# A four-layer graph network on one core: tail rows and the next head's row sent in pieces behind feature loads, and the order of some sigmoids and scalings

## Chip, core and metric

The kernel runs on one core of a Trainium2 chip. The metric is the device time of one execution in microseconds (us); 1734.3 us is the median of three runs of the kernel before, which lie between 1733.95 and 1735.32 us.

## What is computed

The input is a feature matrix `x` of 2708 x 512 and a symmetric 0/1 adjacency matrix `adj` of 2708 x 2708. Four graph layers follow one another, each on a layer norm with relu of the running `x`, and each added to it. The change lies in the third one, graph attention with eight heads of 64 columns:

```python
h = jnp.maximum(_layernorm(x, axis=-1), 0.0)
Wh = jnp.einsum('nd,hdo->hno', h, W)             # 8 heads, 64 columns each
f1 = jnp.einsum('hno,ho->hn', Wh, a1)
f2 = jnp.einsum('hno,ho->hn', Wh, a2)
e = leaky_relu(f1[:, :, None] + f2[:, None, :], negative_slope=0.2)
e = jnp.where(adj[None, :, :] > 0, e, NEG_INF)
attention = softmax(e, axis=-1)
x = x + elu(einsum('hnm,hmo->hno', attention, Wh))   # heads side by side
```

The other three layers are matrix products with `adj` and with 512 x 512 weights. They are untouched.

## The kernel before

**Engines.** TensorE (PE) multiplies matrices, VectorE (DVE) and ScalarE (ACT) work on tiles element by element, GpSimd (POOL) issues one kind of DMA here, and SyncE (SP) issues most of the others. Each engine works through its own list of instructions in order. The lists are written by a recording layer from the order in the source; a call inside `tc.issue_after(x)` is placed behind the instruction `x` in its lists.

**Steps.** The 2708 nodes are cut into `NC` = 22 chunks, 21 of 128 rows and a last one of 20. Attention goes through ten units: unit 0 and unit 1 are head 0 on the first 1408 and the last 1300 columns, units 2 to 7 are heads 1 to 6 on all 2708 columns, units 8 and 9 are head 7, again in two parts. A unit has 22 steps, one for each chunk; units 1 to 8 begin with the chunk of 20 rows. Steps are counted through: unit 0 has steps 0 to 21, unit 1 steps 22 to 43, unit 2 begins with step 44.

**One step.** `scale` (ACT, L1110 and L1112) multiplies the chunk's features `wh` by a factor of each row and writes `whs` (4 buffers). `make` (DVE, L1126) forms the tile `t`, the larger of the head's row `rb` and a value of each partition, times the adjacency; four buffers of it exist (`TILES`), so the DVE may be up to four steps ahead of the PE, and `t` of step s waits until the PE has multiplied `t` of step s-4. `multiply` (PE, L1385) multiplies `whs` by `t` into `av` and, in some steps, `sums`. In the others (17 of the 22 in units 1 to 8) `compare` (ACT, L1144) writes the tile `b` by a steep sigmoid of `t`, and `multiply_sides` adds its product to `sums` one step later. The loop of steps calls `load_wh(s + 6)` where a group of three chunks begins, then `scale(s + 3)`, `make(s + 3)`, `compare(s + 1)`, `multiply(s)` and `multiply_sides(s - 1)`.

**What else runs in steps 1 to 42.** `mask` has POOL load pieces of a stored 0/1 mask (`maskd`, 162 or 176 KB each), two pieces for each half of 17 chunks, into five buffer places that take turns; `count_neighbors` multiplies them (PE, `adj_sums`, L1464) one step after the planned load. A load waits until the product that used its buffers has been done.

**The plan.** `behind(s, f, ...)` has `f` called at the end of step s of the loop. Of these calls the following matter. `load_row1` (SP, L1038) sends one head's row of up to 2708 values to all 128 partitions of `rb` (1354 KB for a whole row; two buffers); unit 1's part is planned at step 10 and unit 2's whole row at step 24. `load_tails` at step 12 loads what the chunk of 20 rows needs in the six heads of units 2 to 7, packed into 120 partitions: besides small pieces, for each head its row on 20 partitions of `tails_row` (L1056, 212 KB each). `exp_tails` (step 20, ACT) and `make_tails` (step 36, DVE, L1074) turn them into one tile of 120 x 2708, which takes the place of `t` in the first step of units 2 to 7. `evict` (ACT, L1429, with SP's L1431) copies a unit's results out after its last step.

`load_wh` (SP, L1096 and L1099) has three buffers of three chunks each. Its DMA for a group waits for the scalings of the group three before it.

Of the kernel before, what the change touches and what calls it, by code (L numbers as in the profile page):

```python
# [14 lines left out]
AF = mybir.ActivationFunctionType  # L15
# [7 lines left out]
R = 128  # L23
# [21 lines left out]
def fast_layers(  # L45
# [36 lines left out]
    nc = tc.nc  # L82
    N, D = x_in.shape
    H, _, O = w2.shape
    NC = -(-N // R)
# [3 lines left out]
    last_rows = N - (NC - 1) * R  # L89
    assert last_rows <= TAIL and TAIL + last_rows <= R  # L90

    def rows(c):
        return min(R, N - c * R)
# [250 lines left out]
    class Fusion:  # L344
# [34 lines left out]
        def multiply(self, i, f, k):  # L379
            if k == 0:  # L380
                self.po[i, f] = ps.tile([P, D], F32, name="fused_ps", tag="ps")
            po = self.po[i, f]
            nc.tensor.matmul(  # L383
                po,
                self.wsT[i][:, k, f * P : (f + 1) * P],
                self.wc[i][:, k, :],
                start=(k == 0),
                stop=(k == NF - 1),
            )
            if k == NF - 1:  # L390
                wf = self.pool.tile([P, D], F32, name="wf", bufs=1)
                nc.scalar.copy(wf, self.po.pop((i, f)))
                nc.gpsimd.dma_start(fused[i][f * P : (f + 1) * P, :], wf)
# [92 lines left out]
    rT = dram.tile([H, NC * R], F32, name="rT")  # L486

    with ExitStack() as ring_ctx:
# [31 lines left out]
        with tc.tile_pool(name="l0", bufs=2) as wk, ExitStack() as ctx_l0:  # L520
            units = [(g, m) for g in range(len(groups)) for m in range(NC)]
# [462 lines left out]
    STEEP = 2.0**62  # L984
# [3 lines left out]
    units = [(h, 0, N) for h in range(H)]  # L988
# [3 lines left out]
    middle = [units[u][0] for u in range(2, len(units) - 2)]  # L992

    def in_tails(u, m):
        return m == NC - 1 and units[u][0] in middle
# [7 lines left out]
    def by_side(u, m):  # L1003
        return 0 < u < len(units) - 1 and m in BY_SIDE
# [14 lines left out]
    eb = at.tile([R, NC, H], F32, name="eb")  # L1019
# [9 lines left out]
    row, weight, wh, whs, acc, sides, made, scaled = {}, {}, {}, {}, {}, {}, [], {}  # L1029
# [17 lines left out]
    def lines_of(h):  # L1047
        i = middle.index(h)
        return slice(i * last_rows, (i + 1) * last_rows)

    def load_tails():
        g, k = where[NC - 1]
        for i, h in enumerate(middle):
            own = lines_of(h)
            src = rT[h : h + 1, :N]
            nc.sync.dma_start(  # L1056
                tails_row[own],
                bass.AP(tensor=src.tensor, offset=src.offset, ap=[[0, last_rows], [1, N]]),
            )
            nc.sync.dma_start(tails_v[own], vT[g][:last_rows, k, :N])  # L1060
            nc.sync.dma_start(tails_f[own, :1], f12[:last_rows, NC - 1, H + h : H + h + 1])
            nc.sync.dma_start(
                tails_w[own, i, :O], whd[(NC - 1) * R :, h * O : (h + 1) * O]
            )
            nc.sync.dma_start(tails_w[own, i, O:], one6[:last_rows])
# [15 lines left out]
        )  # L1081

    GROUP = 3

    def load_wh(s):
        u = steps[s][0]
        h = units[u][0]
        t = at.tile([R, GROUP, O], F32, name="wh", bufs=3)
        ms = [m for v, m in steps[s : s + GROUP] if v == u and not in_tails(u, m)]
        full = [m for m in ms if m < NC - 1]  # L1090
        k = len(full)
        for j, m in enumerate(sorted(ms)):
            wh[u, m] = t[:, j]
        if k:
            src = whd[full[0] * R : (full[0] + k) * R, h * O : (h + 1) * O]
            nc.sync.dma_start(t[:, :k], src.rearrange("(k p) o -> p k o", p=R))  # L1096
        if k < len(ms):
            src = whd[(NC - 1) * R :, h * O : (h + 1) * O]
            nc.sync.dma_start(t[:last_rows, k], src)  # L1099

    def scale(s):

        u, m = steps[s]
        h, q = units[u][0], rows(m)
        if in_tails(u, m):
            whs[s] = tails_w[:LINES, middle.index(h)]
            return
        t = at.tile([R, O + S], F32, name="whs", bufs=4)
        by = ef[:q, m, h : h + 1]
        ins = nc.scalar.activation(t[:q, :O], wh.pop((u, m))[:q], AF.Copy, scale=by)  # L1110
        if not by_side(u, m):
            ins = nc.scalar.activation(t[:q, O:], one6[:q], AF.Copy, scale=by)  # L1112
        scaled[s] = ins.ins
        whs[s] = t[:q]

    def make(s):
        u, m = steps[s]
        h, lo, hi = units[u]
        q = rows(m)
        g, k = where[m]  # L1120
        if in_tails(u, m):
            weight[s] = tails_row[:LINES]
            made.append(made[-1])
            return
        t = at.tile([R, N], F32, name="t2", bufs=TILES)
        ins = nc.vector.scalar_tensor_tensor(  # L1126
            t[:q, : hi - lo],
            row[h][:q, lo:hi],
            ec[:q, m, h : h + 1],
            vT[g][:q, k, lo:hi],  # L1130
            op0=ALU.max,
            op1=ALU.mult,
        )
        weight[s] = t[:q]
        made.append(ins.ins)

    def compare(s):

        u, m = steps[s]
        h, lo, hi = units[u]  # L1140
        q = rows(m)
        if by_side(u, m):
            b = at.tile([R, N], BF16, name="b", bufs=2)
            nc.scalar.activation(  # L1144
                b[:q, : hi - lo],
                weight[s][:, : hi - lo],
                AF.Sigmoid,
                bias=eb[:q, m, h : h + 1],
                scale=STEEP,
            )  # L1150
            sides[s] = b

    l2p = ctx.enter_context(ExitStack())
# [104 lines left out]
    def rows2(c):  # L1258
# [12 lines left out]
        if c == LATE:  # L1271
            load_wh(0)
            load_wh(GROUP)
        if LATE < c <= LATE + 3:
# [14 lines left out]
    tails_row = tails.tile([P, N], F32, name="tails_row")  # L1289
# [121 lines left out]
    def multiply_sides(s):  # L1411

        if s in sides:
            u, m = steps[s]
            h, q = units[u][0], rows(m)
            b = sides.pop(s)[:q]
            at_col = (m * H + h) * 8
            w = parts[:q, at_col : at_col + S]
            four(acc[u][1], sizes_of(u)[1], [(w, b, j) for j in range(4)], s)
# [71 lines left out]
    def behind(s, fn, *args):  # L1491
        plan.setdefault(s, []).append((fn, args))
# [5 lines left out]
    behind(10, load_row1, *units[1])  # L1498
    behind(9, split, EARLY, NC)
    behind(12, load_tails)  # L1500
    behind(20, exp_tails)
    behind(36, make_tails)
    behind(3 * NC, load_l3_weights)
    behind(30, spread_nodes)
    for u in range(2, len(units)):
        if units[u][1] == 0:
            behind(max(1, u - 1) * NC + 2, load_row1, units[u][0], 0, N)
    for u in range(len(units)):
        behind((u + 1) * NC - 1, evict, u, 0)
        behind(min((u + 1) * NC, len(steps) - 1), evict, u, 1)  # L1510
# [34 lines left out]
    for s in range(len(steps)):  # L1545
        if s == (len(units) - 3) * NC + 1:
            tails_ctx.close()
            first3 = ctx.enter_context(
                tc.tile_pool(name="first3", bufs=1, side="right", reuse_waits="tile")
            )  # L1550
            rings3 = [first3]
            b3 = first3.tile([P, D], F32, name="b3")
            nc.sync.dma_start(
                b3, bass.AP(tensor=bias3.tensor, offset=bias3.offset, ap=[[0, P], [1, D]])
            )
            e3_ctx = ctx.enter_context(ExitStack())
            e3 = e3_ctx.enter_context(
                tc.tile_pool(name="e3", bufs=2, side="right", reuse_waits="tile")
            )
        if s + 6 < len(steps) and (s + 6) % NC % GROUP == 0:  # L1560
            load_wh(s + 6)
        if s + 3 < len(steps):
            scale(s + 3)
            make(s + 3)
        if s + 1 < len(steps):
            compare(s + 1)
        multiply(s)
        multiply_sides(s - 1)
        for fn, args in plan.pop(s, ()):
            if fn is load_l3_weights:  # L1570
                with tc.issue_after(row_loads[-1]):
                    fn(*args)
            elif fn in (spread_nodes, split):
                with tc.issue_after(made[s]):
                    fn(*args)
            elif fn is count_neighbors:
                with tc.issue_after(multiplied[s]):
                    fn(*args)
            else:
                fn(*args)  # L1580
# [674 lines left out]
def kernel(tc: tile.TileContext, *args: bass.AP):  # L2255

    nc = tc.nc
    with tc.tile_pool(name="verdict", bufs=1) as pool:
        verdict = pool.tile([1, 1], I32, name="verdict")
        fast_layers(tc, *args, verdict)  # L2260
        odd = nc.values_load(verdict[0:1, 0:1], min_val=0, max_val=P + 1)
        with tc.If(odd > 0):
            general_layers(tc, *args)
# [32 lines left out]
```

## Time and profile before

| | |
|---|---|
| runs of the kernel before | 1733.95, 1734.3, 1735.32 us |
| the profiled execution | 1735.47 us, of which the span of the trace is 1733.6 us; mean granted clock 0.997 |
| PE | busy 1715.0 us (99%) |
| DVE | busy 1307.8 us (75%) |
| ACT | busy 876.5 us (51%) |
| POOL | busy 276.6 us (16%) |
| `t` by L1126, DVE | x214, 511.8 us |
| `b` by L1144, ACT | x136, 308.3 us |
| attention steps | first `t` at 796.2 us, last at 1337.5 us from the span's start |
| mask loads | landed 2.5 to 13.5 us after their issue, median 3.8 us |

Times inside the trace are counted from the start of the span. In the timeline a row is one instruction, or several alike in a row (x and their number), with its start, its length, the engine, the line, the operation, output and inputs, shapes, and in brackets how long the engine was idle ahead of it and what ended that. Starts of neighbours may overlap the ends of the rows before by about 0.1 us, since an engine takes the next instruction in before the last has drained. SPq is SP's queue, whose rows are the issues of DMAs and not their transfers. PEclk is the granted clock of TensorE, 1.00 being full speed.

### The profile page before, as it was taken

To read this page: it belongs to the slowest core of one execution; us is meant where nothing else is said; L and a number is where in the kernel's file an instruction comes from. 1 tells how busy PE (TensorE), PEld (TensorE's weight loads), DVE (VectorE), ACT (ScalarE), POOL (GpSimd) and SP (SyncE) were. 2 spreads that over 40 slices of the span, in tenths; PEclk is the share of its full clock that TensorE was granted. 3 is DMA by queue.
4 is the path that set the end of the run, shared out by engine and by line. 5 is a ranking of instruction groups with operands and counts; after the bars stand their busy time and mean duration, and the time that the engine had idled before them with its cause. 6 is when DMAs were issued, how large, how long until landed. Compare 5 with 4: busy or idle time off the path is not lost.

```text
span 1733.6 us, 29645 instructions
## 1 busy us (share of the span) xinstructions
PE 1715.0 (99%) x11252; PEld 1018.8 (59%) x11252; DVE 1307.8 (75%) x1885; ACT 876.5 (51%) x1565; POOL 276.6 (16%) x314
## 2 busy tenths in 40 slices
PE   9999999999999999999899999999999999999998
PEld 5567777744458888644344433433434555588886
DVE  7759889855556666877799999999999777633334
ACT  5447767622224510265497888888894666400000
POOL 1003323312121111366320000000001222100000
PEclk9999999999999999999999999999999999999999
DMA  9336666444464421344771221122022444312221
GB/s 319 116 118 198 204 205 190 141 116 123 123 161 147 163 92 49 118 132 140 205 208 29 61 64 45 28 65 66 16 67 74 141 139 136 101 46 100 74 73 42
DMA packets 180846, 200.96 MB, mean 116 GB/s; under 512 B 86320, under 2 KB 117488, under 8 KB 179677
## 3 DMA queue, kind: packets, MB, share of 16 engines
q1 hardware_dynamic: 144156, 131.47, 27.0%
q10 hardware_dynamic: 28888, 45.68, 7.0%
q0 software_dynamic: 7648, 21.82, 3.9%
q8 instruction: 90, 1.47, 0.4%
q14 instruction: 64, 0.52, 0.1%
HBM read 123.42 MB, written 67.15 MB: 110 GB/s over the span
## 4 chain that ended last, share of the span: by engine, by line
PE 75%; DVE 14%; issue 6%; ACT 2%; DMA 2%; POOL 1%; DVEq 0%; SPq 0%; ACTq 0%; POOLq 0%
PE acc L437 37%; DVE t L1126 11%; PE nb_ps L193 8%; PE av L1385 8%; PE wh_ps L193 4%; PE self_ps L193 4%; PE line_ps L193 4%; PE h_ps L193 3%; PE hT_ps L258 2%; PE sums L1385 2%; PE fused_ps L383 2%; ACT b L1144 1%; DMA x<-maskd 1%; DMA x<-in_x 1%; PE av_ps L1320 1%
## 5 line engine op out<-in xcount | busy, mean ns | idle before, releaser
L1126 DVE SCALAR_TENSOR_TENSOR t<-rb,ec,vT 128x2708 f32<-128x2708 f32 (+2 forms) x214 | 511.8, 2465 | 13.2 <-PE sums L1385 10.4
L1385 PE MATMUL av<-t,whs 128*32 128x451 f32 (+4 forms) x4432 | 424.0, 515 | 5.6 <-DVE t L1126 2.8
L437 PE MATMUL acc<-halves,kt 128*128 128x512 f32 x1848 | 423.6, 390 | 1.0 <-DVE kt L928 1.0
L437 PEld LDWEIGHTS acc<-halves,kt 128*128 128x128 f32 x1848 | 346.0, 188 | 75.3 <-DVE kt L928 2.6
L1144 ACT ACTIVATE b<-t,eb 128x2708 bf16<-128x2708 f32 (+2 forms) x136 | 308.3, 2267 | 46.5 <-DVE t L1126 46.3
L1385 PEld LDWEIGHTS av<-t,whs 128*32 128x32 f32 (+1 forms) x4432 | 146.0, 110 | 200.0 <-issue 156.9
L437 PE MATMUL acc<-halves,ar 128*128 128x512 f32 x924 | 243.7, 414 | 0.0
L437 PEld LDWEIGHTS acc<-halves,ar 128*128 128x128 f32 x924 | 172.6, 188 | 58.2 <-issue 20.3
L928 DVE SCALAR_TENSOR_TENSOR kt<-lastr,index,vT 128x512 fp32r<-128x512 int16 (+3 forms) x154 | 108.5, 719 | 63.3 <-PE acc L437 62.1
L1613 DVE CAST kt<-vT 128x512 fp32r<-128x512 uint8 (+3 forms) x154 | 56.3, 368 | 130.8 <-PE acc L437 130.7
L1337 POOL TENSOR_SCALAR z<-y 128x512 f32<-128x512 f32 x22 | 44.2, 2007 | 559.0 <-DVE y L1330 548.3
L570 DVE TENSOR_TENSOR_SCAN cum<-ai,deg 128x512 int16<-128x512 int32 (+2 forms) x110 | 128.1, 1168 | 0.0
L235 ACT ACTIVATE ln_rs<-ln_mv,eps 128x1 f32<-128x1 f32 x88 | 25.6, 294 | 195.0 <-DVE ln_mv L230 192.8
L613 ACT ACTIVATE cum<-cum,limit 128x512 int16<-128x512 int16 (+3 forms) x132 | 88.0, 667 | 57.1 <-DVE deg L578 54.8
L1110 ACT ACTIVATE whs<-wh,ef 128x64 f32<-128x64 f32 x214 | 72.1, 342 | 51.2 <-PE sums L1385 21.0
L228 DVE BATCH_NORM_STATS2 ln_st<-x 128x6 f32<-128x512 f32 x88 | 60.4, 688 | 48.1 <-DMA x<-x 33.9
L920 ACT CAST hT<-vT 128x704 bf16<-128x704 uint8 (+1 forms) x68 | 50.8, 757 | 63.2 <-DMA maskd<-hT 51.7
L193 PE MATMUL h_ps<-w0s,hT 128*128 128x512 f32 x168 | 76.0, 595 | 0.6 <-DVE ln_rs L237 0.3
L193 PE MATMUL wh_ps<-w2s,hT 128*128 128x512 f32 x168 | 75.8, 594 | 0.0
L564 ACT ACTIVATE ar<-ai 128x512 fp32r<-128x512 int32 (+2 forms) x132 | 75.0, 568 | 1.6 <-DMA ai<-in_adj 1.1
L193 PE MATMUL self_ps<-wfs,hT 128*128 128x512 f32 x168 | 75.7, 593 | 0.0
L193 PE MATMUL nb_ps<-wfn,hT 128*128 128x512 f32 x168 | 75.6, 593 | 0.0
(223 smaller groups left out, 1957.0 us busy)
## 6 DMA issues: line engine op xcount, KB each, us to landing
x<-x SPq DMA_DIRECT2D x105, 256.0 KB
ai<-in_adj SPq DMA_DIRECT2D x84, 256.0 KB
x<-x ACTq DMA_DIRECT2D x84, 256.0 KB
x<-in_x SPq DMA_DIRECT2D x42, 256.0 KB
rb<-rT SPq DMA_DIRECT2D x7, 1354.0 KB
maskd<-hT ACTq DMA_DIRECT2D x34, 176.0 KB
wh<-whd SPq DMA_DIRECT2D x62, 96.0 KB
packed<-two POOLq DMA_DIRECT2D x44, 128.0 KB, 3.1
```

Of the source, the lines that this page charges most:

```text
L193: nc.tensor.matmul(po[:n], lhsT[:, f, :n], w[:, f, :], start=(f == 0), stop=(f == NF - 1))
L228: nc.vector.bn_stats(st[:n], xc[:n])
L437: nc.tensor.matmul(acc[:R], weight[:, k * R : (k + 1) * R], parts[:, i, :], start=(m == 0 and i == 0), stop=(m == NC - 1),)
L564: nc.scalar.activation(ar[:, :gw], ai[:, :gw], AF.Square, accum_out=squares[:R, m, g : g + 1])
L570: nc.vector.tensor_tensor_scan(cum[:n, :gw], ai[:n, :gw], ai[:n, :gw], 0.0 if g == 0 else deg[:n, m : m + 1], op0=ALU.add, op1=ALU.max,)
L613: nc.scalar.activation(cum[:n, :gw], cum[:n, :gw], AF.Sign, bias=limit[:n], scale=-1.0, accum_out=signs[:n, m, g : g + 1],)
L928: nc.vector.scalar_tensor_tensor(by_chunk(kt, cs), lastr[:, cs[0] * R : (cs[-1] + 1) * R].rearrange("p (c r) -> p c r", r=R), index[:R, m ...
L1110: ins = nc.scalar.activation(t[:q, :O], wh.pop((u, m))[:q], AF.Copy, scale=by)
L1126: ins = nc.vector.scalar_tensor_tensor(t[:q, : hi - lo], row[h][:q, lo:hi], ec[:q, m, h : h + 1], vT[g][:q, k, lo:hi], op0=ALU.max, op1=AL ...
L1144: nc.scalar.activation(b[:q, : hi - lo], weight[s][:, : hi - lo], AF.Sigmoid, bias=eb[:q, m, h : h + 1], scale=STEEP,)
L1385: ins = nc.tensor.matmul(p[j * S : (j + 1) * S, : b - a], lhsT, rhs[:, part * size + a : part * size + b], start=(s % NC == 0), stop=(s % ...
L1613: nc.vector.tensor_copy(by_chunk(kt, cs), pattern(m, cs))
```

## The change

Four edits, all in the plan of the attention layer:

1. The six `tails_row` loads leave `load_tails` and become `load_tail_row(h)`. They are planned at steps 12, 16, 19, 22, 25 and 28, each behind the feature load (`load_wh`) that the same step issues.
2. Unit 2's row is loaded in three parts of 900, 904 and 904 columns (450 to 452 KB), at steps 31, 34 and 37, each again behind that step's feature load. Later units' rows are planned where they were.
3. `make_tails` is placed on the DVE behind `t` of step 36. In the list of the built program its instruction moves from between `t` of steps 25 and 26 to eleven tiles later.
4. In unit 1 the sigmoid of a step is placed behind the scaling of the next step's chunk. In the built program the ACT list at the end of unit 0 was: table load, sigmoid of step 23, three copies of `evict`, sigmoid of step 24, scalings of steps 22 to 28. It becomes: scalings of steps 22, 23 and 24, table load, sigmoid of step 23, two copies of `evict`, scaling of 25, third copy, scaling of 26, sigmoid of 24, scalings of 27 and 28.

The lists of PE and POOL are the same in both programs; SP's differs by the loads named, and two copies of `evict` at the end of unit 1 change places on ACT.

```diff
+    def load_tail_row(h):
+        src = rT[h : h + 1, :N]
+        nc.sync.dma_start(
+            tails_row[lines_of(h)],
+            bass.AP(tensor=src.tensor, offset=src.offset, ap=[[0, last_rows], [1, N]]),
+        )
+
     def load_tails():
         g, k = where[NC - 1]
         for i, h in enumerate(middle):
             own = lines_of(h)
-            src = rT[h : h + 1, :N]
-            nc.sync.dma_start(
-                tails_row[own],
-                bass.AP(tensor=src.tensor, offset=src.offset, ap=[[0, last_rows], [1, N]]),
-            )
             nc.sync.dma_start(tails_v[own], vT[g][:last_rows, k, :N])
...
+    wh_loads = {}
 
     def load_wh(s):
...
-            nc.sync.dma_start(t[:, :k], src.rearrange("(k p) o -> p k o", p=R))
+            ins = nc.sync.dma_start(t[:, :k], src.rearrange("(k p) o -> p k o", p=R))
+            wh_loads[s] = ins.ins
...
         if by_side(u, m):
             b = at.tile([R, N], BF16, name="b", bufs=2)
-            nc.scalar.activation(
...
-            )
+            with ExitStack() as behind:
+                if u == 1:
+                    behind.enter_context(tc.issue_after(scaled[min(s + 1, 2 * NC - 1)]))
+                nc.scalar.activation(
...
+                )
             sides[s] = b
...
-    for u in range(2, len(units)):
+    for u in range(3, len(units)):
         if units[u][1] == 0:
-            behind(max(1, u - 1) * NC + 2, load_row1, units[u][0], 0, N)
+            behind((u - 1) * NC + 2, load_row1, units[u][0], 0, N)
+    at_groups = [
+        s for s in range(9, 2 * NC) if (s + 6) % NC % GROUP == 0 and s + 6 != NC - 1
+    ]
+    for i, h in enumerate(middle):
+        behind(at_groups[1 + i], load_tail_row, h)
+    for i in range(3):
+        lo, hi = (N // 4 * j // 3 * 4 for j in (i, i + 1))
+        behind(at_groups[7 + i], load_row1, units[2][0], lo, hi)
...
-            elif fn in (spread_nodes, split):
+            elif fn is load_tail_row or (fn is load_row1 and NC < s < 2 * NC):
+                with tc.issue_after(wh_loads[s + 6]):
+                    fn(*args)
+            elif fn in (spread_nodes, split, make_tails):
                 with tc.issue_after(made[s]):
                     fn(*args)
```

More of the change, by code (lines that the diff above doesn't have):

```diff
@@ L1143, in compare @@
             b = at.tile([R, N], BF16, name="b", bufs=2)
[L1144 to L1149, printed above, removed]
-            )
+            with ExitStack() as behind:
+                if u == 1:
+                    behind.enter_context(tc.issue_after(scaled[min(s + 1, 2 * NC - 1)]))
+                nc.scalar.activation(
+                    b[:q, : hi - lo],
+                    weight[s][:, : hi - lo],
+                    AF.Sigmoid,
+                    bias=eb[:q, m, h : h + 1],
+                    scale=STEEP,
+                )
             sides[s] = b
```

## The prediction

> **What bounds the kernel now.** The page gives PE 99% busy and the DVE 75%, over stages with different limits. In the stage that the change touches I looked for the engine that never pauses, and found it in the DVE's timeline from the end of unit 0 on:
>
> ```profile
> 848.99 1.56 DVE L1126 SCALAR_TENSOR_TENSOR t<-rb,ec,vT 20x1300 f32<-20x1300 f32 x1 [0.24 <-PE sums L1385]
> 850.77 1.57 DVE L1126 SCALAR_TENSOR_TENSOR t<-rb,ec,vT 128x1300 f32<-128x1300 f32 x1 [0.21 <-PE sums L1385]
> 854.03 1.57 DVE L1126 SCALAR_TENSOR_TENSOR t<-rb,ec,vT 128x1300 f32<-128x1300 f32 x1 [1.69 <-PE sums L1385]
> 858.05 1.57 DVE L1126 SCALAR_TENSOR_TENSOR t<-rb,ec,vT 128x1300 f32<-128x1300 f32 x1 [2.45 <-PE sums L1385]
> 859.54 3.03 DVE L1074 SCALAR_TENSOR_TENSOR tails_row<-tails_row,tails_f,tails_v 120x2708 f32<-120x2708 f32 x1
> 863.60 1.57 DVE L1126 SCALAR_TENSOR_TENSOR t<-rb,ec,vT 128x1300 f32<-128x1300 f32 x1 [1.03 <-PE sums L1385]
> 866.24 3.07 DVE L1126 SCALAR_TENSOR_TENSOR t<-rb,ec,vT 128x1300 f32<-128x1300 f32 x2 [1.06 <-PE av L1385]
> 869.59 445.47 DVE L1126 SCALAR_TENSOR_TENSOR t<-rb,ec,vT 128x1300 f32<-128x1300 f32 x174 [0.28 <-PE sums L1385]
> ```
>
> These are `t` of steps 22 to 28, `make_tails`, and from step 29 on 174 tiles without a gap: from 869.59 to 1315 us the DVE alone sets the pace. Whatever time it is idle before 869.59 comes back in full at the end, and an instruction moved into the gapless stretch costs its length. The idle times in brackets sum to 0.24 + 0.21 + 1.69 + 2.45 + 1.03 + 1.06 + 0.28 = 6.96 us. All wait for the PE to free a `t` buffer, so next the PE's timeline (columns as above):
>
> ```profile
> 848.74 1.36 PE L1385 MATMUL av<-t,whs 128*32 128x352 f32 x16
> 849.92 0.77 PE L1385 MATMUL sums<-t,whs 128*32 128x352 f32 x8
> ...
> 851.88 0.32 PE L1464 MATMUL adj_sums<-mask,parts 128*24 128x352 bf16 x2 [1.05 <-DMA mask<-maskd]
> ...
> 854.19 0.31 PE L1464 MATMUL adj_sums<-x,parts 128*24 128x325 bf16 x2 [0.21 <-DMA x<-maskd]
> 855.76 0.31 PE L1464 MATMUL adj_sums<-x,parts 128*24 128x325 bf16 x2 [1.26 <-DMA x<-maskd]
> ...
> 860.06 2.39 PE L1385 MATMUL av<-t,whs 20*32 20x325 f32 x16 [1.82 <-ACT whs L1110]
> ```
>
> Three waits for late masks (2.52 us), one for a scaling on ACT (1.82 us). Then SP's queue and ACT, for what was late:
>
> ```profile
> 837.58 0.37 SPq L1038 DMA_DIRECT2D rb<-rT  x1
> 837.99 3.77 SPq L1056 DMA_DIRECT2D tails_row<-rT  x6
> ```
> ```profile
> 852.38 1.38 ACT L1144 ACTIVATE b<-t,eb 128x1300 bf16<-128x1300 f32 x1 [1.70 <-DVE t L1126]
> 856.87 1.04 ACT L1429 COPY out<-av 128x352 f32<-128x352 f32 x2 [3.11 <-PE av L1385]
> 858.05 0.45 ACT L1429 COPY out<-sums 128x352 f32<-128x352 f32 x1
> 858.40 1.38 ACT L1144 ACTIVATE b<-t,eb 128x1300 bf16<-128x1300 f32 x1
> 859.68 1.05 ACT L1110 ACTIVATE whs<-wh,ef 20x64 f32<-20x64 f32 x4
> ```
>
> 650 KB of unit 1's row and six times 212 KB, 1.92 MB, are issued within 4 us. A mask load lands after 3.8 us (median), the worst after 13.5: the pair that POOL issued at 841.7 is the one that the PE waits for at 854.2 and 855.8. And step 22's scaling stands behind two sigmoids and three copies that wait for step 21. The windows show the third loss, the clock:
>
> ```profile
> 840.00:850.00 10.00, 10.00 (x152) 4.27 (x146) 8.96 (x6) 3.28 (x11) 3.81 (x7) 1.00 1.01 221
> 850.00:860.00 10.00, 5.72 (x72) 2.11 (x64) 5.65 (x5) 4.91 (x8) 2.25 (x5) 0.98 0.72 181
> 860.00:870.00 10.00, 9.94 (x108) 3.79 (x112) 7.63 (x5) 3.61 (x11) 4.83 (x9) 0.68 0.99 323
> ```
>
> (busy us of PE, PEld, DVE, ACT, POOL, then clock, DMA share, GB/s). After the waits the clock is 0.68 for 10 us, and matmuls of 325 columns run 2.39 us for sixteen where they later take 1.28.
>
> **Tail rows in pieces.** No bytes are added; each piece now stands behind a feature load, and that behind the scalings that free its buffer. SP is late against its plan at 837.6 (the PE is in step 13, the row was planned for 10), so the first pieces still come quickly. The first follows the row at 838. The second waits through its feature load for the scaling of step 17, which ran at 839.5, the third for step 20's (845.2), the fourth for step 21's (847.1), the last two for those of 24 and 27, about 853 and 859.5 by the schedule below. So I expect pieces at about 838, 840.5, 846, 848, 853.5 and 860: by 842 there are 650 + 2 x 212 = 1.07 MB instead of 1.92. If the delay goes with the burst, the worst landing falls from 13.5 to 3.8 + 9.7 x 1.07 / 1.92 = 9.2 us. Between issue and use lie 12.5 us in step 20 (837.99 to 850.52 before any wait), and for the pair issued at 841.7, due at about 852.4 once step 20 does not wait, 10.7 us. So the mask waits go, with 1.5 us to spare. Bounds: all 2.52 us of PE time, or none.
>
> **Sigmoids behind scalings.** Step 22's scaling needs a `whs` buffer that step 18 frees (849.0), so it is done by 849.7 instead of after 859.68, and the table load (1.28 us, idle time before) now runs at about 853. Behind the waiting sigmoid of step 23 stand only copies and the scaling of 25, which the PE needs at 858.9 and gets at about 856.9. The 1.82 us go. In the steady part of unit 1 the order is the same.
>
> **DVE without the waits.** Step 20 begins at 850.52 + 0.14 (its mask product) = 850.66; like its neighbours it is over 1.95 us later, so `t` of 24 starts at 852.7, idle 0.35. Step 21 begins 1.77 + 0.14 later, 852.57: `t` of 25 at 854.6, idle 0.34. Step 22 begins at 854.49, ends at 856.3: `t` of 26 at 856.4, idle 0.21. From there tiles follow at 1.48 us. Idle left: 0.24 + 0.21 + 0.35 + 0.34 + 0.21 = 1.35; gain 6.96 - 1.35 = 5.6 us. Cross-check: `t` of 29 starts at 856.4 + 3 x 1.48 = 860.8, and 2.94 us of `make_tails` (its pitch in the stream) are still to do, 863.8 against 869.6: 5.8. I take 5.7.
>
> **`make_tails` later.** It was hidden in idle time; now it is 3.03 us in the gapless stretch, and the sum has it. Queued behind it are `t` of 37 and on. `t` of 29 was written at 871.16 and read at 873.48, a lead of 2.3 us that a PE step of 1.43 us hardly changes; so the PE waits some 1.2 us once, which costs nothing as the DVE is the bound. Its data land near 863, it runs near 872, first use is step 44 near 887.
>
> **Row in thirds.** The last part leaves SP at about 873.5; `t` of 45 needs it at 891.85 - 5.8 = 886. The whole row of 1.35 MB went out inside 862 to 868. Cover: 12 us against at most 6.
>
> Sum: the profiled 1735.47 becomes 1729.8. That run lies 1.17 us above the median, so I say 1734.3 - 5.7 = **1728.6 us**. A change under 0.2%, 3.5 us, is about what a measurement here can't tell from none.
>
> **Rivals.** *Masks still late.* Over half of the burst stays. If the landing stays near 12 us, the PE still waits 1.3 us or so and some of the slow clock stays: half the gain, 1731.5. For it: 9.2 against 10.7 is thin, and pieces three and four follow 2 us apart. Against: the last four are spread over 14 us.
>
> *The clock drops again* behind the 1.2 us pause near 877: a stretch like the old one (0.68 over 10 us, 3.2 us lost) that the DVE feels if its four tiles are used up; gain 5.7 - 3.2, 1731.8. Against: just behind `make_tails` the DVE has the most empty buffers ahead, about 4 us. The rows show a drop after waits of 1.05, 0.21, 1.26 and 1.82 us within 9 us, none after a lone 0.65 us at 1334. The Trainium skill (TensorE: Matmul & The Clock Gate, Part 1: The HAM clock gate) has the clock halve only after an idle window of about 3.4 us; by that rule this rival would be out, but the trace differs, its longest single wait being 1.82, and the trace decides.
>
> *Unit 1 starved of DMA (slower).* The row's 1.35 MB used to move while the PE ran slowly. Now it moves inside unit 1, with masks needed every 1.48 us. From 838 to 888 the queues moved 11.74 MB in 50 us, 235 GB/s; now it is the same in 44.3, 265 GB/s. At the 204 GB/s of 838 to 860 it takes 57.5 us, 13.2 more; the DVE absorbs 4 us of a late PE, so 13.2 - 4 - 5.7 = 3.5 slower, 1737.8. It decides below 11.74 / (44.3 + 5.7 + 4) = 217 GB/s. Against: 860 to 870 ran at 323 with row and masks together. The Trainium skill (DMA: Bandwidth & Descriptors, Bandwidth) says to batch DMAs to 1 MiB or more for 75% of peak, which speaks against thirds; an estimate by its fit of 2 us and 436 GB/s is 9.1 us for three parts and 5.1 for one. No run here shows parts of that size.
>
> *The PE is the bound after all*: then all its waits (4.34) and the clock (3.2) come back, 1726.8. Against: the DVE has no gap.
>
> **Chances.** Forecast 0.66, late masks 0.13 (half of it beyond 0.2%), clock 0.06, starved 0.09, PE 0.04, nothing at all 0.02. Faster 0.66 + 0.065 + 0.04, 0.76; same 0.15; slower 0.09. Range: from the PE's case to the clock's with 0.7 on top for its unknown size, 1726.8 to 1732.5; outside lie the starved case and the rest, about 0.15. The forecast's own range is 1727.9 to 1729.6.
>
> **What would show it.** Right: no PE wait for `maskd` or `whs` between 848 and 860, clock 1.00 in 860 to 870, landing at most about 10 us, DVE gapless from about 856, `make_tails` in the stream near 872, `t` of 45 near 886. Wrong: a mask wait in unit 1, a `t` waiting for `rb`, or DVE idle time after 860.

## The result, and the profile after

| | before | after |
|---|---|---|
| median of 22 runs each on one chip | 1735.91 us | 1732.43 us (1730.32 to 1736.74) |
| ratio, 95% interval | | 0.998 [0.9974, 0.9987] |
| profiled execution, span | 1735.47, 1733.6 us | 1731.39, 1729.6 us |

The change is worth 1735.91 - 1732.43 = 3.5 us (2.3 to 4.5 by the interval), and 4.1 us between the two profiled executions; 5.7 were forecast. It is faster, but by some three fifths of what the prediction said. One of the 22 executions before took 1959.31 us, far off the rest; without it the median is 1735.89 us.

The DVE's timeline of the kernel after, from `t` of step 22 on, in the columns of the prediction's first block (start, length, engine, line, operation, tiles, shapes, idle time before and what ended it):

```profile
848.71 1.56 DVE L1130 SCALAR_TENSOR_TENSOR t<-rb,ec,vT 20x1300 f32<-20x1300 f32 x1 [0.24 <-PE sums L1392]
850.49 1.57 DVE L1130 SCALAR_TENSOR_TENSOR t<-rb,ec,vT 128x1300 f32<-128x1300 f32 x1 [0.22 <-PE sums L1392]
852.41 1.57 DVE L1130 SCALAR_TENSOR_TENSOR t<-rb,ec,vT 128x1300 f32<-128x1300 f32 x1 [0.35 <-PE sums L1392]
854.45 1.57 DVE L1130 SCALAR_TENSOR_TENSOR t<-rb,ec,vT 128x1300 f32<-128x1300 f32 x1 [0.47 <-PE sums L1392]
856.48 4.54 DVE L1130 SCALAR_TENSOR_TENSOR t<-rb,ec,vT 128x1300 f32<-128x1300 f32 x3 [0.46 <-PE sums L1392]
862.54 11.96 DVE L1130 SCALAR_TENSOR_TENSOR t<-rb,ec,vT 128x1300 f32<-128x1300 f32 x8 [1.52 <-PE sums L1392]
874.42 3.03 DVE L1076 SCALAR_TENSOR_TENSOR tails_row<-tails_row,tails_f,tails_v 120x2708 f32<-120x2708 f32 x1
877.37 433.59 DVE L1130 SCALAR_TENSOR_TENSOR t<-rb,ec,vT 128x1300 f32<-128x1300 f32 x166
```

The idle times of 1.69, 2.45, 1.03 and 1.06 us are gone and `make_tails` stands in the gapless stretch. The sum is 0.24 + 0.22 + 0.35 + 0.47 + 0.46 + 1.52 = 3.26 us, where 6.96 stood before and 1.35 were forecast. The 3.70 us that went, and 0.28 us by which `t` of 22 starts earlier, make 3.98 of the 4.08 us between the two profiled executions.

What the 1.52 us before 862.54 waits for is on the PE. Its only waits from 848 to 880 are these two:

```profile
860.53 0.31 PE L1471 MATMUL adj_sums<-mask,parts 128*24 128x325 bf16 x2 [1.25 <-DMA mask<-maskd]
...
878.98 1.30 PE L1392 MATMUL av<-t,whs 128*32 128x325 f32 x16 [0.80 <-DVE t L1130]
```

The second is the pause behind `make_tails`, forecast at 1.2 us and free. The first is a mask again, in step 24 this time. SP issued the fifth tail row just ahead of that mask's load on POOL:

```profile
853.26 0.47 SPq L1053 DMA_DIRECT2D tails_row<-rT  x1
```
```profile
853.95 0.56 POOL L1458 DMA_DIRECT2D mask<-maskd  x1 [2.54 <-PE av L1392]
```

The load issued at 853.95 landed at 860.49, 6.54 us later. And the windows (busy us of PE, PEld, DVE, ACT, POOL, then clock, DMA share, GB/s):

```profile
850.00:860.00 10.00, 9.28 (x138) 3.62 (x131) 8.50 (x7) 7.48 (x14) 4.88 (x9) 1.00 0.89 227
860.00:870.00 10.00, 9.47 (x158) 6.17 (x161) 8.48 (x7) 7.75 (x13) 5.95 (x11) 1.00 0.95 265
870.00:880.00 10.00, 9.20 (x155) 5.69 (x149) 10.00 (x7) 7.71 (x12) 5.42 (x10) 1.00 1.00 352
```

The clock of 0.68 is gone in this execution. So one loss is left over in the stage, and the question for the experiments is why it is there, and whether it explains the whole shortfall.

### The profile page after: what moved, and what is told of

Read it like the earlier page. It is cut to its first block, busy times and chain, and to the rows that moved or that the text cites. A ratio compares the mean times of both kernels' runs of the same rounds, so it can differ in the third digit from the quotient of the medians.

```text
span 1729.6 us, 29656 instructions
## 1 busy us (share of the span) xinstructions
PE 1710.5 (99%) x11252; PEld 1017.9 (59%) x11252; DVE 1308.2 (76%) x1885; ACT 876.6 (51%) x1565; POOL 275.5 (16%) x314
## 4 chain that ended last, share of the span: by engine, by line
PE 78%; DVE 12%; issue 5%; DMA 2%; ACT 1%; POOL 1%; DVEq 0%; SPq 0%; ACTq 0%; POOLq 0%
PE acc L437 37%; PE av L1392 10%; DVE t L1130 10%; PE nb_ps L193 8%; PE self_ps L193 4%; PE wh_ps L193 4%; PE line_ps L193 4%; PE h_ps L193 3%; PE sums L1392 2%; PE hT_ps L258 2%; PE fused_ps L383 2%; ACT b L1151 1%; DMA x<-in_x 1%; PE av_ps L1327 1%; DMA x<-maskd 0%
```

## Experiments

Each kernel was timed against the kernel before on its own chip; the before medians were 1736.17 (first four), 1735.74 (second four) and 1736.03 us (last four). The line numbers in the rows are each kernel's own.

**Which edits act.** The first kernel has edits 1 to 3 and not the fourth:

```diff
-            with ExitStack() as behind:
-                if u == 1:
-                    behind.enter_context(tc.issue_after(scaled[min(s + 1, 2 * NC - 1)]))
+            with ExitStack():
```

> Edits 1 to 3 without the fourth (no rule that places unit 1's sigmoids behind scalings). In this program the ACT list already has step 22's scaling ahead of the sigmoids, as in the changed kernel; only the scaling of step 24 stands behind the sigmoid of step 23 instead of ahead of it. Theory A (the gain is that of the loads; the order on ACT follows from them): no wait for whs longer than 0.3 us, time within 0.7 us of the changed kernel, about 4 us below the kernel before. Theory B (the fourth edit is what takes away the 1.82 us wait for whs): that wait comes back, about 2 us of the 4 are lost.

Measured: 1731.6 us, ratio 0.9974 [0.9962, 0.9985], span 1728.0. Its idle times are 0.24, 0.21, 0.35, 0.47 and 0.46, and from step 26 on there is no gap (DVE's timeline):

```profile
856.44 16.47 DVE L1130 SCALAR_TENSOR_TENSOR t<-rb,ec,vT 128x1300 f32<-128x1300 f32 x11 [0.46 <-PE sums L1390]
```

This is the forecast schedule, and the profiled gain of 5.6 us in the span is the forecast one. (The profile is of the fastest of the seven executions; by the medians the gain is 4.6 us.) Its built ACT list also has the scaling of step 22 early (848.72), and SP issues unit 0's results ahead of the fifth tail row. The mask load issued at 853.90 landed after 4.08 us, and there was no wait. The second kernel is the kernel before with edit 4 alone:

> The kernel before with the fourth edit alone: six tail rows at once, whole row, make_tails early. Theory A: the three mask waits (2.5 us) stay, the scaling of step 22 now stands behind the three copies of evict, and the PE waits some 1.2 us for it; 0 to 1 us below the kernel before. Theory B: the wait for whs is gone, 2 us or more below the kernel before.

Measured: 1735.79 us, ratio 1.0002 [0.9993, 1.0011]. The scaling of step 22, the first of four in this ACT row, stays late, and so does the PE:

```profile
859.12 1.06 ACT L1110 ACTIVATE whs<-wh,ef 20x64 f32<-20x64 f32 x4 [1.80 <-DMA wh<-whd]
```
```profile
859.52 2.39 PE L1388 MATMUL av<-t,whs 20*32 20x325 f32 x16 [2.17 <-ACT whs L1110]
```

The scaling's wait ends on its feature load, which SP issued at 844.64 behind the six tail rows: by 859.1, that is up to 14.5 us. In the kernel before two sigmoids and three copies stood over this wait and hid it. So the fourth edit alone takes nothing away; it is the rows in pieces that bring the scaling forward.

**Sizes and places.** The third kernel sends the tail rows later still (and `make_tails` behind 38, the thirds at 37, 38 and 41):

```diff
-        behind(at_groups[1 + i], load_tail_row, h)
+        behind((12, 16, 25, 28, 31, 34)[i], load_tail_row, h)
```

> The changed kernel with tail rows at steps 12, 16, 25, 28, 31, 34, thirds of the row at 37, 38, 41 and make_tails behind step 38: no tail rows leave SP between 842 and 852 us. Theory A (the remaining mask wait of 1.25 us at 860.5 comes from loads that SP sends between 845 and 859): masks of that time land in 6 us or less, the wait is gone, 1.5 us below the changed kernel (profiled about 1729.9). Theory C (that mask load is late because POOL issues it late, 3.4 us after its buffer was free): the wait stays, as the changed kernel. If the third part of the row comes too late for step 45, a DVE wait for rb of up to 2 us shows instead.

Measured: 1733.08 us, ratio 0.9981 [0.9972, 0.999]. No row leaves SP between 840.6 and 852.7. The mask load of 853.48 landed after 3.13 us, although the third tail row (852.79) went out just ahead of it, and the wait at 860 is gone. But the DVE has idle times of 1.06 us at 858.65 and 0.28 at 862.20: the clock was halved from 855.88 to 859.30, with no PE wait over 0.15 us since 846. `make_tails` then waited 1.33 us for the last tail row. The fourth kernel sends unit 2's row whole, by the line that stood before:

```diff
-    for u in range(3, len(units)):
+    for u in range(2, len(units)):
         if units[u][1] == 0:
-            behind((u - 1) * NC + 2, load_row1, units[u][0], 0, N)
+            behind(max(1, u - 1) * NC + 2, load_row1, units[u][0], 0, N)
```

> The changed kernel with unit 2's row whole at step 24, as before; in this program it leaves SP ahead of unit 0's results, near 853 us. Theory A: 1.35 MB ahead of the masks of unit 1's first steps; landings of 10 us and more against a lead of 8.4, mask waits of 3 to 5 us at 857 to 865, 3 to 5 us above the changed kernel. Theory C: as the changed kernel, within 0.7 us.

Measured: 1735.03 us, ratio 0.9993 [0.9984, 1.0002]. The 1.35 MB left SP at 847.88, ahead of unit 0's results, and the feature load behind those, issued at 863.36, was late for ACT:

```profile
867.96 0.35 ACT L1114 ACTIVATE whs<-wh,ef 128x64 f32<-128x64 f32 x1 [3.40 <-DMA wh<-whd]
```

This came out as 2.64 us of DVE idle time at 869.61, and here too the clock was halved, from 855.70 to 859.11. The mask waits that were expected did not come. The whole row at this place gives back two thirds of the gain. But the edit changes the size and the time of the load together: the row leaves SP 17 us ahead of the first third of the changed kernel (864.91). Which of the two costs the gain is not shown, since a whole row at the place of the first third was not run. The Trainium skill (DMA: Bandwidth & Descriptors, Bandwidth) asks for 1 MiB and more per transfer; this pair of runs decides neither for nor against that.

**The clock drops without a wait.** In these two profiles the drop follows steps 21 and 22, which both multiply the 20-row chunk (about 4 us together, from 852 on in the changed kernel). In the profiles here the clock is at half for 3.41, 6.83 or 10.24 us in this stage, that is for one, two or three windows of 3.41 us, and the windows lie at another phase in each execution. Theory D: when one such window holds hardly anything but matmuls on 20 partitions, the next has half the clock. Four kernels test it, and the landing. Two repeat a step's matmuls, so that its chunk is summed three times: step 21 (20 partitions) or, as the control, step 20 (128 partitions), on top of the first kernel:

```diff
+        for e in (s - 1, s - 1, s) if s == NC - 1 else (s,):      # control: NC - 2
-        ins = four(acc[u][0], half, [(cols[j % 2], t, j // 2) for j in range(4)], s)
+            ins = four(acc[u][0], half, [(cols[j % 2], t, j // 2) for j in range(4)], e)
```

> The rows alone, and TensorE does the eight matmuls of av and four of sums of step 21 (20 partitions) three times; the sums then hold chunk 21 of unit 0 three times, which the reference doesn't. Adds some 3.9 us of matmuls on 20 partitions with no wait between them: steps 21 and 22 are then 7.8 us of them. Theory D: at least one whole window of 3.41 us lies in it in every execution, whatever its phase, so the granted clock is at half for one or two windows (3.4 or 6.8 us) behind it, with no PE wait ahead of the drop; this costs 1.3 to 2.7 us more than the 3.9 us of added matmuls: 1.3 to 2.7 us slower than the kernel that repeats a 128-row step. Rival E: the clock stays at 1.00, and the time is that of the kernel that repeats a 128-row step, within 0.4 us.

> The control: the rows alone, and the same number of matmuls of the same width is added, at step 20 (128 partitions) instead of step 21; the sums then hold chunk 20 of unit 0 three times. Theory D: no window is full of 20-row matmuls any more often than in the rows alone, the granted clock stays at 1.00 in most executions, and the kernel is slower than the rows alone by at most the added 3.9 us (about 1735.5), less by what PE has spare before step 26. Rival E: as slow as the kernel that repeats the 20-row step, within 0.4 us.

Measured: 1739.05 us (ratio 1.0018 [1.0009, 1.0027]) and 1735.23 (0.9999 [0.999, 1.0008]), 3.8 us apart for the same number and width of matmuls. The windows of the kernel that repeats 20 rows, cut where its clock changes:

```profile
852.08:855.49 3.41, 3.41 (x52) 1.43 (x48) 1.18 (x1) 2.40 (x3) 1.64 (x3) 1.00 0.80 185
855.49:865.73 10.24, 10.24 (x80) 3.15 (x76) 3.58 (x3) 2.50 (x7) 2.17 (x4) 0.50 0.64 182
```

and of the control:

```profile
857.07:860.48 3.41, 3.41 (x52) 1.19 (x48) 2.56 (x2) 2.97 (x6) 1.95 (x4) 1.00 0.79 182
860.48:863.90 3.42, 3.42 (x34) 1.46 (x36) 2.31 (x2) 0.70 (x2) 1.37 (x3) 0.50 0.97 289
```

PE is busy throughout the first of the two windows of each. In the first kernel 20-row matmuls run from 851.68 to 862.5 and the clock is half for three windows; in the control they run from 856.48 to 860.50, one window lies in that, and one has half the clock; no drop follows the windows of its added 128-row matmuls. The expectation for the control was a clock of 1.00 in most executions, and that failed: over the span ten of its eleven have 0.998 or less, against three of seven in the first kernel. Why the drop came so often there is not shown. The size for the 20 rows was underestimated (1.3 to 2.7): half the clock makes the 20-row stretch itself longer, which fills the next window too.

The other two of this group take one cause away each. The first puts unit 0's 20-row chunk at step 18 (again without edit 4):

```diff
-        for m in ((NC - 1, *range(NC - 1)) if 0 < u < len(units) - 1 else range(NC))
+        for m in (
+            (NC - 1, *range(NC - 1))
+            if 0 < u < len(units) - 1
+            else (*range(NC - 4), NC - 1, *range(NC - 4, NC - 1))
+            if u == 0
+            else range(NC)
+        )
```

> The kernel with the rows alone (edits 1 to 3), and unit 0 takes its 20-row chunk at step 18 instead of step 21, so that steps 21 and 22 no longer both multiply 20 partitions. Theory D (the clock is halved for one window of 3.41 us when such a window lies wholly in matmuls of 20 partitions; step 21 and step 22 together are 3.95 us): a single 20-row step is 1.9 to 2 us, so no window is full of it, and the granted clock stays at 1.00 from 845 to 880 us in every execution. DVE stands as with the rows alone (five idle times of 0.2 to 0.5 us, none from step 26 on), the span is about 1728.0, the median at or up to 0.5 us under that of the rows alone (0.9974). Rival E (the drop follows from something else that comes round at that time, such as the loads of the rows): the drop is seen in some executions as before, and nothing changes; the profile's clock may then stand at 0.50 for 3.41 us between 852 and 862.

Measured: 1730.29 us, ratio 0.9972 [0.9959, 0.9984], six executions from 1729.56 to 1731.3, the clock over the span 0.999 or 1.0 in each, no drop in the profile. The second has all four edits and moves only the fifth tail row:

```diff
-                with tc.issue_after(wh_loads[s + 6]):
+                last = fn is load_tail_row and args[0] == middle[4]
+                with tc.issue_after(results[0, 1] if last else wh_loads[s + 6]):
```

(`results[0, 1]` is the last DMA of unit 0's `evict`.)

> The changed kernel whole, and only the fifth tail row (212 KB, issued at 853.26) leaves SP behind unit 0's results instead. Theory A (the 1.25 us mask wait of PE at 860.5 is that row's landing: the mask load issued at 853.95 took 6.54 us beside it): the load lands in 4.0 to 4.7 us, by 858.7, PE has no mask wait at step 24, DVE works without a gap from about 856.5, the 1.52 us at 862.5 is gone, and the kernel is 1.3 to 1.5 us faster than the changed one: ratio 0.9972 to 0.9976. Rival B (the order of sigmoids and scalings on ACT, by which the changed kernel differs from the rows alone too, sets the wait): the wait of 1.2 to 1.5 us stays, and the ratio stays at 0.998.

Measured: 1732.23 us, ratio 0.9979 [0.9969, 0.9988]. The landing came as theory A has it: 855.00 to 859.24, 4.24 us, and no mask wait. POOL's issue of that load (KB, us to landing), in the changed kernel and then in this one:

```profile
mask<-maskd POOLq DMA_DIRECT2D x1, 162.5 KB, 6.5
```
```profile
mask<-maskd POOLq DMA_DIRECT2D x1, 162.5 KB, 4.2
```

The gain did not come, and the ratio is the one of rival B, though the mask wait that it went with is gone: in this profile the clock was halved from 857.84 to 861.25. The three executions with a clock of 0.999 over the span took 1729.59 to 1730.27 us, the seven with 0.998 or less 1731.24 to 1734.11. In all eleven profiles here of kernels with the tail rows in pieces, 0.999 goes with no drop in this stage and 0.998 or less with one.

**Both causes, singly and together.** The last four ran on one chip.

> The changed kernel once more, for its trace and beside the three that follow on one chip. Theory D (clock halved for 3.41 us where most of such a window, at a phase that differs between executions, lies in the 20-row steps 21 and 22) and theory A (mask wait of 1.25 us behind the fifth tail row): ratio 0.998 as before; the executions fall into two groups about 1.2 us apart, by whether the granted clock over the whole span is 0.999 or more, or lower; if this profile has the drop, it lies between 855 and 860, and the mask wait of PE at 860 is partly inside it.

Measured: 1732.81 us, ratio 0.998 [0.9972, 0.9989]. This execution of the changed kernel has the drop and not the mask wait (its windows, then two rows of the PE):

```profile
853.30:856.71 3.41, 3.41 (x51) 1.34 (x52) 2.94 (x2) 3.38 (x5) 1.93 (x4) 1.00 0.84 243
856.71:860.12 3.41, 3.41 (x32) 1.00 (x28) 1.72 (x2) 2.67 (x6) 1.86 (x4) 0.50 0.98 233
```
```profile
853.24 1.39 PE L1392 MATMUL av<-t,whs 20*32 20x352 f32 x16
...
855.40 1.30 PE L1392 MATMUL av<-t,whs 20*32 20x325 f32 x16
```

The fifth row is where it was, and the mask load beside it took 6.09 us (854.78 to 860.88), but the PE, at half the clock, came to it later. The DVE's idle times from `t` of 22 on are 0.24, 0.22, 0.35, 0.47, 0.85 and 1.08, together 3.21 us, as much as the 3.26 with the wait. Of the 33 executions of the changed kernel 22 have a clock over the span of 0.998 or less; their median is 1732.89 us, that of the other eleven 1731.53, and the ranges overlap.

The order alone, on the changed kernel (the diff is that of the order above):

> The changed kernel whole, and only unit 0's 20-row chunk at step 18 instead of 21. Theory D: the clock stays at 1.00 in every execution (0.999 or more over the span), so the median falls by the share of executions with the drop (13 of 22) times its 1.2 to 1.3 us, some 0.7 us, to ratio 0.9973 to 0.9977, and the executions lie closer together; the mask wait of about 1.2 us near 860 stays, so it stays about 1.3 us slower than the kernel with both edits. Rival (the gain seen with the rows alone and this order came from no fifth row ahead of the results, not from the clock): ratio 0.998 and executions with a clock of 0.998 or less.

Measured: 1733.29 us, ratio 0.9979 [0.997, 0.9988]. No drop in the profile, and eight of eleven executions at 0.999, not all of them. The expected 0.7 us did not come. In the profile the whole mask wait stands there without the drop (and eleven executions from 1729.54 to 1735.44 us could hardly show 0.7 us):

```profile
862.33 0.31 PE L1477 MATMUL adj_sums<-mask,parts 128*24 128x325 bf16 x2 [1.60 <-DMA mask<-maskd]
```

Both edits on the changed kernel:

> The changed kernel with the fifth tail row behind unit 0's results and the 20-row chunk at step 18: theories A and D together. No mask wait near 860, no clock drop, DVE without a gap from step 26 on: span 1727.8 to 1728.4, ratio 0.9966 to 0.9972, 5 to 6 us under before, which is the size that was forecast for the change. If the fourth edit (sigmoids of unit 1 behind scalings) is worth anything, this is faster than the same two edits without it (1730.29 us at a before of 1735.74); theory: the same within 0.5 us.

Measured: 1730.6 us, ratio 0.9967 [0.9954, 0.998], five executions from 1729.4 to 1730.65, all at 0.999. DVE's timeline:

```profile
857.03 16.47 DVE L1136 SCALAR_TENSOR_TENSOR t<-rb,ec,vT 128x1300 f32<-128x1300 f32 x11 [0.35 <-PE sums L1398]
873.42 3.03 DVE L1082 SCALAR_TENSOR_TENSOR tails_row<-tails_row,tails_f,tails_v 120x2708 f32<-120x2708 f32 x1
```

The idle times are 0.35, 0.35, 0.35, 0.34 and 0.35, together 1.74 us. On this chip ten of eleven executions of the changed kernel are slower than the slowest of these five. With the order and without edit 4 the ratio was 0.9972, with an interval that covers this one: no worth of edit 4 shows.

The profiles agree when the stage is taken alone: from the first `t` of the attention to the first row behind the gapless stretch the DVE takes 518.8 us in the kernel before, 514.7 and 514.5 in the two profiles of the changed kernel, 514.8 with the fifth row moved, 514.5 with the order changed, and 512.5 with both. The profile of edits 1 to 3, which has neither loss, also gives 512.5.

The order alone, on the kernel before:

> The kernel before, and only unit 0's 20-row chunk at step 18. Theory D with the waits of before: its drop near 860 (6.83 us) came from a window filled by the 20-row step 21 and the 1.82 us whs wait behind it; now step 21 multiplies 128 rows, and what is left in one stretch is the wait of 1.8 us and the 20-row step 22 of 2 us, so the drop comes in fewer executions or for 3.41 us. The waits themselves stay (mask 2.5 us in all, whs 1.8 us): 0.3 to 1.2 us faster than before, ratio 0.9993 to 0.9998. Rival: the drop belongs to the waits alone, and nothing changes (ratio 1.000).

Measured: 1736.4 us, ratio 0.9999 [0.999, 1.0008], the rival's figure. The clock was halved twice all the same. The first time it was for 3.41 us, behind a window with mask waits of 0.21 and 1.75 us and no 20-row matmul:

```profile
852.29:855.71 3.42, 1.46 (x24) 0.54 (x16) 2.21 (x2) 1.38 (x1) 0.55 (x1) 1.00 0.75 204
855.71:859.12 3.41, 3.41 (x30) 1.36 (x24) 0.00 (x0) 0.91 (x2) 0.55 (x1) 0.50 0.52 174
```

The second time it was for 6.83 us, behind a window of 3.41 us with 1.49 us busy (a whs wait of 1.92). In the first profile of the changed kernel the window from 857.70 to 861.11, with its mask wait, has 2.16 us busy and no drop follows. So in the kernel before the waits suffice for a drop.

## Why the prediction was right in part, and where it failed

Right: what bounds the stage. Idle time of the DVE ahead of the gapless stretch came back nearly one for one (3.70 us of idle and 0.28 of an earlier start, of 4.08). Right as well: the pieces (837.67, 840.51, 845.73, 847.64, 853.26 and 863.03, forecast 838 to 860); the worst landing, 9.2 us, forecast 9.2 (8.3 to 9.5 in the other kernels with the rows in pieces, so the exact agreement is luck); the last third at 872.92; `make_tails` at 874.42 instead of 872, with 0.80 us of PE wait and a clock of 1.00 behind it. No tile waited for a row: every idle time of the DVE ahead of a `t` ended on the PE. So "starved of DMA" and "the clock drops again" near 877 did not come; from 838 to 882 us the queues moved 265 GB/s, as reckoned, where 217 was the point.

Right in effect, wrong in cause: "The 1.82 us go." They went, but not by the fourth edit. The prediction took the `whs` buffer, free at 849.0, as all that the scaling needed; its feature load lay in the same burst as the masks, as the run with edit 4 alone shows.

Wrong: "So the mask waits go, with 1.5 us to spare." The waits in steps 19 and 20 went. The lead of 10.7 us that the landing was held against is that of a mask issued at 841.7, in unit 0, where a step is over 1.9 us. In unit 1 steps of about 1.4 us use the same buffers up. The load of 853.95 was due at 860.53 - 1.25 = 859.28: a lead of 5.3 us, against a landing of 6.54, well under the worst case that was reckoned with. That put back 1.52 us of idle time. The fifth tail row, 0.7 us ahead of it on SP, made the difference: the same load took 6.54, 6.09 and 6.66 us with the row there (two profiles of the changed kernel, one with the order), and 4.08, 4.24 and 3.29 us with the row behind the results (edits 1 to 3, the fifth row moved, both). It seems to have done so on top of the rows of 845.73 and 847.64 (the mask load of 850.85, issued ahead of the fifth row, took 7.51 us): where these two came later, in the kernel with the late tail rows, a row at the same place left the landing at 3.13. The prediction had all three rows at their times and set none of them against the masks of unit 1. The rival "masks still late" (1731.5) named the right kind of loss, in the wrong unit.

Wrong too: the clock. The prediction tied every drop to PE waits. In two of three executions of the changed kernel the clock over the span is lower than where no drop shows, and the one profile of these has the drop with no wait ahead of it, behind the two 20-row steps. By the idle times of the two profiles it costs as much as the mask wait does (3.21 and 3.26 us); that the executions with the lower clock are 1.4 us slower in the median is not explained by these two. A row for it was there: of the drop at 860 of the kernel before, the 1.82 us wait and the 20-row steps 21 and 22 on both sides of it were candidates alike, and only the wait was counted (with the order changed in the kernel before the drops stayed, so there the waits do suffice). In the two profiles of the changed kernel the phase of the windows decided which of the two came (in the first, the 20-row matmuls fall into two windows, with 1.90 and 1.78 us in each, and no drop follows; in the second 3.15 us fall into one), and the drop hid the wait. Taking one away gave 0.9979 both times, taking both 0.9967; the intervals of these ratios overlap, and what carries the point is the ten of eleven executions on one chip and the 512.5 us of the stage.

The terms: forecast idle 1.35 us, measured 3.26. Of the 1.91 between, 1.52 is the wait (or, in other executions, about as much by the drop), 0.13 and 0.25 are two terms taken at 0.34 and 0.21 that measured 0.47 and 0.46. With both causes gone the kernel is 5.4 us under before (1736.03 - 1730.6), close to the 5.7. In absolute time, 1732.43 is 3.8 us over the forecast 1728.6; 2.2 of these is the gain (5.7 - 3.5), and 1.6 is the base: the median of before over 22 runs was 1735.91 and not the 1734.3 of three.

Open: POOL issued the late mask 3.1 us after the one before it, in every kernel with the rows in pieces (851.69 and 854.78, for instance), idle 2.5 us by the row "PE av". Why it waits so long was not settled; without that pause the load would have had its time. Of the 2.2 us by which the two edits together beat the changed kernel on one chip, 514.5 - 512.5 = 2.0 lie in the attention by the profiles, and the idle times explain 3.21 - 1.74 = 1.5 of them; the rest was not followed up.

## What to carry to other kernels

Hold a landing time against the lead of the stage in which the buffer is used, not of the one in which it was first seen: where steps get shorter, every lead shrinks with them, and three loads of 212 KB within 8 us were enough here. When two causes of loss lie on the same microseconds, removing one brings up the other; try both together before either is called worthless. And where the executions of one kernel differ by several us, one profile may not show the cause: take a second.

## What the hardware showed that was not expected

The granted clock halved without any PE wait over 0.15 us. It changed in windows of 3.41 us. A window with 3.15 us of matmuls on 20 partitions and 0.26 on 128 was followed by one at half the clock (853.30 to 856.71 in the second profile of the changed kernel; three in a row where such matmuls went on to 862.5). So was one with 2.72 and 0.69 us (854.42 to 857.84 with the fifth row moved), but not one with 2.23 and 1.18 us (851.44 to 854.85 with edits 1 to 3, its phase counted back from the half clock that begins at 1725.25). These times are worked out from the starts and lengths of PE's rows. The limit for this kernel lies between the two. With no 20-row matmul at all, 1.46 us on 128 partitions was followed by a drop (852.29 to 855.71 in the kernel before with the order changed), so by these windows the 20-row ones count for something, but for less. The Trainium skill (TensorE: Matmul & The Clock Gate, Part 1: The HAM clock gate) ties the drop to an idle window of some 3.4 us; the length agrees with the 3.41 us here, the idleness does not: PE was busy for all of one such window, and for 1.46 us of another.
